# One two-bank PSUM tile for the sums of a feed-forward pair, and one VectorE operation of 1024 columns to read it

## The chip, the cores and the metric

The kernel runs on one core of a Trainium2 chip. The metric is device time of one execution in microseconds (us), as the median of several runs. A core has five engines with a queue each: TensorE (PE in the profile; its weight loads are listed apart as PEld), VectorE (DVE), ScalarE (ACT), GpSimd (POOL) and SyncE (SP). TensorE writes its results into PSUM, an accumulator memory of 128 partitions that is divided into banks; in this kernel a bank holds 512 fp32 numbers per partition. VectorE and ScalarE read PSUM; everything else lives in SBUF, and DMA queues carry it from and to HBM. Engines wait for one another through semaphores.

## The reference

The input x has the shape (4, 512, 128, 64): batch, time, F = 128 positions, H = 64 channels, in fp32. All arithmetic is fp32. There are two layers. The first is a chain of four residual blocks for each batch, with d = 128 * 64 = 8192 features per time step:

```python
xn = layernorm(x.reshape(b, t, d), g, b)
k, v, r = xn @ Wk, xn @ Wv, sigmoid(xn @ Wr)     # d -> 64
state = scan over time: decay * state + k * v
x = x + (r * states) @ Wo                        # 64 -> d
x = x + gelu(conv_F(layernorm(x)) + b)           # 3 taps over F, 64 -> 64 channels
x = x + layernorm(causal_depthwise_conv_T(layernorm(x)))   # 3 taps over time
x = x + (gelu(x @ W1 + b1) @ W2 + b2)            # 64 -> 256 -> 64, at each position
```

The second layer splits x into a moving average over 25 steps and the rest, takes the rest through a real Fourier transform over the 512 steps, mixes 128 modes with complex weights, transforms back, and adds the average. The change does not touch it.

## The kernel before, in words

The first layer holds data with features on partitions: a chunk is 128 features by 512 time steps, and a pair of chunks is a tile of [128, 2, 512]. One batch is 32 pairs (`NPR`). Six generator functions make the stages of a batch `b`:

- `project` (J, L325): k, v and r for all pairs, eight matmuls (L408) per pair.
- `scan` (Z, L421): the scan over time and the moments that follow from it. It is a chain of small steps that go from TensorE to VectorE or ScalarE and back.
- `attend_and_convolve` (A, L516): adds the attention's output (L530, L532), convolves over F (L565), and sums the pair and its squares over features with four matmuls into a PSUM bank `st` (`add_up`, L247 to L252, called from L598). `st` lives from the third pair of A to its end.
- `convolve_time` (C, L647): the time convolution on VectorE and ScalarE, with the same kind of sums in a bank of its own.
- `open_feed` (O, L707): spreads two columns of statistics to rows and makes the first two inputs of the feed-forward.
- `feed_forward` (F, L715): for each pair, and each quarter `q` of the 256 hidden channels, `widen` (four matmuls L733, then a gelu on ScalarE, L738) and `narrow` (four matmuls L746 that add into two PSUM banks). After the last quarter, VectorE adds bias and residual (L759), and `store` transposes the result (eight transposes L765), copies it out of PSUM (L773 or L778) and sends it to HBM. The store of a pair comes `lag` pairs after its sums: one in batches 0 and 1, two in batches 2 and 3. Batches 0 and 1 keep the result of the sums in `x4t` with three buffers of [128, 512], batches 2 and 3 in a spare tile of two chunks.

Three helpers recur in scan, C and O. `rows` (L281) turns a column of statistics into a row by four matmuls (`spread`, L239, L242) into a bank, and copies it out on ScalarE (L286). `finish` (L257) copies the sums of `add_up` to SBUF on ScalarE (L260), picks columns with small matmuls (L264) and copies them on VectorE (L269). `moments` (L271) makes mean and scale of them. The bank that `rows`, `finish` and the scan write is an argument: `of_a` takes half of the pool `ps_a`, `of_p` a bank of the pool `ps_p`.

[...]`ps_a`, `ps_c` and `ps_m` have one tile of two banks each; `ps_s` has one bank, which `st` of stage A and the second sum `pb` of the feed-forward share; `ps_p` has one bank, for `of_p`'s users (scan of batch 1, rows and sums of C and O in batches 0 to 2, and the preparation in batch 0) and the feed-forward's first sum `p`.

TensorE's order is written by hand: `in_turn` (L824) steps two chains of stages in turn, each by its share of the work: first batch 0's Z and A against batch 1's J and Z; then C0 against A1; O0 and F0 against J2 and Z2; C1 against A2; O1 and F1 against J3 and Z3; C2 against A3; O2 and F2 against C3 and O3; and F3 alone. A flag, `free_s`, keeps a feed-forward from starting while `st` is in use, and `feeding` keeps A's `st` from starting in a feed-forward. The order on the other engines is made by a scheduler when the kernel is built, and the builder puts in the semaphores, by the tiles that instructions read and write.

Of the kernel before, what the change touches and what calls it, by code (L numbers as in the profile page):

```python
# [10 lines left out]
F32 = mybir.dt.float32  # L11
AF = mybir.ActivationFunctionType
ALU = mybir.AluOpType
PSUM = bass.MemoryType.PSUM
# [66 lines left out]
def layer0(ctx, tc, dram, x, xt, vecs, wkvr, wo, wdec, wconv, fbias, w1, fb1, w2, fb2, x4):  # L81
# [16 lines left out]
    tiny = ctx.enter_context(tc.tile_pool(name="tiny", bufs=2))  # L98
    ps_a = ctx.enter_context(tc.tile_pool(name="ps_a", bufs=1, space=PSUM))
    ps_c = ctx.enter_context(tc.tile_pool(name="ps_c", bufs=1, space=PSUM))  # L100
    ps_s = ctx.enter_context(tc.tile_pool(name="ps_s", bufs=1, space=PSUM))
    ps_m = ctx.enter_context(tc.tile_pool(name="ps_m", bufs=1, space=PSUM))
    ps_p = ctx.enter_context(tc.tile_pool(name="ps_p", bufs=1, space=PSUM))

    def two(pool, tag):
        return pool.tile([P, 2, SL], F32, tag=tag, name=tag)
# [198 lines left out]
        return two(ps_a, "a")[:, 0, :]  # L305

    def of_p():
        return ps_p.tile([P, SL], F32, tag="p", name="p")

    projected = {}  # L310
    scanned = {}
# [13 lines left out]
    def project(b):  # L325
        pa = two(ps_m, "m") if b == 1 else two(ps_a, "a")
        held[0] = b == 1
        if b == 0:
            psum_w = ps_p.tile([P, SL], F32, tag="p", name="psum_w")
        stt = rowp.tile([P, NT, NS, 6], F32, tag="stt", name="stt")  # L330
        def token_major(i, xk):
            s, h = i // 2, i % 2 * 2
            nc.sync.dma_start(
                xk, x[b, h * P : (h + 2) * P, s * SL : (s + 1) * SL].rearrange("(t p) d -> p t d", p=P)
            )
            return xk

        def statistics(i, xk):
            s, h = i // 2, i % 2 * 2
            for t in range(2):  # L340
                stats = nc.vector.bn_stats(stt[:, h + t, s, :], xk[:, t, :])
                if b > 1:

                    tc.keep_in_program_order(stats)

        def weights(i):

            if i < NPR:
                w = spare("wx", 4 * S + SL).rearrange("p k n -> p (k n)")[:, 0 : 16 * S]
                w = w.rearrange("p (c s) -> p c s", c=4)  # L350
                nc.sync.dma_start(w, wkvr[2 * i : 2 * i + 4, :, 0 : 4 * S].rearrange("c p s -> p c s"))
                for k in range(2):
                    ws[i + k] = w[:, 2 * k : 2 * k + 2, :]

        def scale_weights(i, wq, pinned=False):
            for j in range(2):
                w = wq[:, j, 0 : 3 * S]
                scaled = nc.vector.tensor_scalar_mul(w, w, vec[:, G1, 2 * i + j : 2 * i + j + 1])
                if pinned:
                    tc.keep_in_program_order(scaled)  # L360

        ws, xps, xks = {}, {}, {}
        if b > 1:
            weights(0)
            for k in range(2):
                scale_weights(k, ws[k], True)
            xps[0] = load_x(b, 0)
        for i in range(NPR):
            first, last = i == 0, i == NPR - 1
            if b > 1:  # L370


                xks[i] = token_major(i, two(bk, "sq" if i % 2 else "x2"))
                if i % 2 == 0:
                    weights(i + 2)
                if not last:
                    xps[i + 1] = load_x(b, i + 1)
                wq, xp = ws.pop(i), xps.pop(i)
                for k in (i - 2, NPR - 2, NPR - 1) if last else (i - 2,):
                    if k in xks:  # L380
                        statistics(k, xks.pop(k))
            else:
                if unscanned[0]:

                    wq, xk = two(fr, "x1")[:, :, 0 : 4 * S + 3], spare("z", SL)
                else:

                    both = spare("wx", 4 * S + SL)
                    wq, xk = both[:, :, 0 : 4 * S], both[:, :, 4 * S :]
                n = 4 * S + 2 * (b == 0)  # L390
                nc.sync.dma_start(wq[:, :, 0 : n], wkvr[2 * i : 2 * i + 2, :, 0 : n].rearrange("c p s -> p c s"))
                xp = load_x(b, i)
                statistics(i, token_major(i, xk))
            if b == 0:
                nc.gpsimd.memset(wq[:, :, n:], 1.0)
                for j in range(2):
                    c = 2 * i + j

                    w = wq[:, j, :]
                    nc.tensor.matmul(  # L400
                        psum_w[0 : S + 2, 0 : 4 * S + 3], lhsT=w[:, 3 * S : 4 * S + 2], rhs=w,
                        start=c == 0, stop=c == NCH - 1,
                    )
            if b < 2:
                scale_weights(i, wq)
            for j in range(2):
                for k in range(2):
                    nc.tensor.matmul(  # L408
                        pa[:, k, :], lhsT=wq[:, j, k * P : (k + 1) * P], rhs=xp[:, j, :],
                        start=first and j == 0, stop=last and j == 1,  # L410
                    )
                if b > 1 and j == 1 and i + 2 < NPR:
                    scale_weights(i + 2, ws[i + 2], True)
                yield 1.0
        kvrg = rowp.tile([P, 2, SL], F32, tag="kvrg", name="kvrg")
        nc.scalar.copy(kvrg, pa)
        held[0] = False
        projected[b] = (kvrg, stt, psum_w) if b == 0 else (kvrg, stt)
# [97 lines left out]
    def attend_and_convolve(b):  # L516
# [62 lines left out]
        for i in range(NPR + 3):  # L579

            while begin[attend_and_convolve] < b + (min(i, 3) - 3) / 4:
                yield BLOCKED
            if i < 2:
                scaled(i)
            if i < NPR:
                attend(i)
                yield 1.0
            if 1 < i < NPR + 2:
                convolve(i - 2)
                yield 5.0  # L590
            while i == 3 and feeding[0]:
                yield BLOCKED
            if i == 3:
                st = ps_s.tile([P, SL], F32, tag="s", name="st")
                free_s[0] = False
            if i > 2:
                add_up(st, i - 3, *waiting.pop(i - 3), i == 3, i == NPR + 2)
                yield 1.0  # L598
            if b == 0 and i >= NPR and i < NPR + 2:
                begin[attend_and_convolve] = b + (0.25 if i == NPR else 0.75)  # L600
# [113 lines left out]

    def feed_forward(b):  # L715
        x3s = opened.pop(b)
        mids, x4s, obs, sums2 = {}, {}, {}, {}
        lag = 1 if b + 2 < B else 2
        turn = [0]
        while not free_s[0]:  # L720
# [17 lines left out]
            nc.scalar.activation(mid, pm, AF.Gelu_apprx_tanh, bias=fb1_sb[:, q : q + 1])  # L738

        def narrow(i, q):  # L740
            if q == 0:
                sums2[i] = of_p(), ps_s.tile([P, SL], F32, tag="s", name="pb")
            mid = mids.pop((i, q))
            for h in range(2):
                for j in range(2):
                    nc.tensor.matmul(  # L746
                        sums2[i][j][halves[h], :], lhsT=w2_sb[halves[j], q, :], rhs=mid[halves[j], h, :],
                        start=q == 0, stop=q == 3,
                    )
            if q < 3:  # L750
                return
            x3 = x3s.pop(i)
            if lag > 1:
                pair = spare("wx", 4 * S + SL)[:, :, 0:SL]
                x4s[i] = [pair[:, j, :] for j in range(2)]
            else:
                x4s[i] = [bk.tile([P, SL], F32, tag="x4t", name="x4t", bufs=3) for _ in range(2)]
            for j, pa in enumerate(sums2.pop(i)):
                nc.vector.scalar_tensor_tensor(x4s[i][j], pa, fb2_sb, x3[:, j, :], ALU.add, ALU.add)  # L759

        def store(i):
            pt = unit()
            for j, x4t in enumerate(x4s.pop(i)):
                for t in range(NT):
                    nc.tensor.transpose(pt[:, j, t * P : (t + 1) * P], x4t[:, t * P : (t + 1) * P], ident)  # L765
            s = i // 2
            if i % 2 == 0:
                obs[s] = bk.tile([P, NT, SL], F32, tag="ob", name="ob")
            o = obs[s][:, :, i % 2 * 2 * P : (i % 2 + 1) * 2 * P].rearrange("p t (j w) -> p j t w", j=2)
            pt = pt.rearrange("p j (t w) -> p j t w", t=NT)  # L770
            if i % 2:
                for h in range(2):
                    nc.scalar.copy(o[:, :, :, halves[1 - h]], pt[:, :, :, halves[h]])  # L773
                nc.gpsimd.dma_start(
                    x4[b][:, s * SL : (s + 1) * SL].rearrange("(t p) d -> p t d", p=P), obs.pop(s)
                )
            else:
                nc.scalar.copy(o, pt)  # L778
# [419 lines left out]
```

## Time and profile before

| | before |
|---|---|
| median of 3 runs | 3731.04 us (3726.51 to 3733.54) |
| profiled execution | 3727.17 us |
| its span in the profile | 3725.4 us |
| mean granted TensorE clock | 0.983 |
| TensorE busy | 3519.4 us, 94% |
| VectorE busy | 2671.6 us, 72% |
| ScalarE busy | 1779.8 us, 48% |
| GpSimd busy | 450.4 us, 12% |

A line such as "L759 DVE SCALAR_TENSOR_TENSOR x4t<-p,fb_sb,x 128x512" names the line of the kernel, the engine, the operation, the tile that is written and those that are read (by the program's names, which tiles share when they share memory), and its shape in partitions by columns. "Idle before" is how long the engine had nothing to do ahead of it, with the work that released it behind the arrow. The granted clock is the share of TensorE's full rate that the profile's clock records show. The stages follow one another in this way, in us from the start of the span: projections of batch 0 and what precedes A0 to about 430; scan of batch 1 beside A0 from about 446; C0 beside A1 from about 548 to 794; F0 beside J2 from 830, and its last pairs, with the scan of batch 2, to 1235; C1 beside A2 to 1462; F1 beside J3, and its last pairs to 1888; C2 beside A3 to 2114; F2 beside C3 from 2130 to about 2402, and the rest of F2 to 2490; F3 to 2745; the second layer to 3726.

### The profile page before, as it was taken

To read this page: it belongs to the slowest core of one execution; us is meant where nothing else is said; L and a number is where in the kernel's file an instruction comes from. 1 tells how busy PE (TensorE), PEld (TensorE's weight loads), DVE (VectorE), ACT (ScalarE), POOL (GpSimd) and SP (SyncE) were. 2 spreads that over 40 slices of the span, in tenths; PEclk is the share of its full clock that TensorE was granted. 3 is DMA by queue.
4 is the path that set the end of the run, shared out by engine and by line. 5 is a ranking of instruction groups with operands and counts; after the bars stand their busy time and mean duration, and the time that the engine had idled before them with its cause. 6 is when DMAs were issued, how large, how long until landed. Compare 5 with 4: busy or idle time off the path is not lost. (4 is left out here: it accounts for less than half of the span.)

```text
span 3725.4 us, 53006 instructions
## 1 busy us (share of the span) xinstructions
PE 3519.4 (94%) x20041; PEld 1366.8 (37%) x20041; DVE 2671.6 (72%) x3498; ACT 1779.8 (48%) x2331; POOL 450.4 (12%) x654
## 2 busy tenths in 40 slices
PE   9999999989999999999999989899989999899998
PEld 4433322224333223433322333333323843328433
DVE  4455569976777896677789699946658277792677
ACT  0013346546666565566656588878855200152100
POOL 0000012220011211001122122100000000001000
PEclk9999999999999999999999999999999999999999
DMA  9867647777885787788478677645569479994687
GB/s 313 282 211 243 227 154 270 254 264 259 293 295 176 249 275 267 265 292 296 167 240 286 210 245 268 233 154 194 199 202 285 154 231 295 300 295 167 214 286 263
DMA packets 427223, 910.29 MB, mean 244 GB/s; under 512 B 32728, under 2 KB 83160, under 8 KB 422872
## 3 DMA queue, kind: packets, MB, share of 16 engines
q1 hardware_dynamic: 353136, 636.92, 52.7%
q0 software_dynamic: 71680, 268.46, 19.8%
q8 instruction: 160, 2.62, 0.3%
q10 hardware_dynamic: 2152, 1.51, 0.1%
q14 instruction: 95, 0.78, 0.1%
HBM read 638.26 MB, written 268.50 MB: 243 GB/s over the span
## 5 line engine op out<-in xcount | busy, mean ns | idle before, releaser
L746 PE MATMUL p<-mid,w_sb 64*64 64x512 f32 x2048 | 560.8, 595 | 24.0 <-DVE wx L759 23.3
L746 PE MATMUL pb<-mid,w_sb 64*64 64x512 f32 x2048 | 533.4, 595 | 0.0
L738 ACT ACTIVATE mid<-c,fb_sb 128x1024 f32<-128x1024 f32 x256 | 284.6, 1112 | 94.5 <-PE c L733 92.3
L738 ACT ACTIVATE mid<-m,fb_sb 128x1024 f32<-128x1024 f32 x256 | 285.0, 1113 | 91.2 <-PE m L733 89.7
L733 PE MATMUL c<-x,w_sb 64*64 64x512 f32 x2016 | 281.6, 606 | 11.1 <-ACT mid L738 7.0
L733 PE MATMUL m<-x,w_sb 64*64 64x512 f32 x2016 | 283.3, 609 | 5.6 <-ACT ob L778 3.4
L746 PEld LDWEIGHTS p<-mid,w_sb 64*64 64x64 f32 x2048 | 160.4, 134 | 289.6 <-issue 244.0
L408 PE MATMUL a<-xp,wx 128*128 128x512 f32 x512 | 240.0, 613 | 6.6 <-issue 6.6
L1044 ACT COPY two<-a 128x512 f32<-128x512 f32 x64 | 37.5, 587 | 428.4 <-PE a L1039 428.4
L1067 PE MATMUL b<-xin,avg_sb 128*128 128x512 f32 x512 | 230.8, 593 | 3.3 <-DVE xin L1073 3.3
L1073 DVE TENSOR_TENSOR xin<-b,pm 128x512 f32<-128x512 f32 x256 | 159.1, 684 | 99.2 <-PE b L1070 84.3
L571 ACT ACTIVATE sq<-x 128x1024 f32<-128x1024 f32 x128 | 135.2, 1056 | 181.4 <-DVE x L568 181.3
L626 DVE SCALAR_TENSOR_TENSOR to<-kd,vec,to 128x510 f32<-128x510 f32 (+1 forms) x272 | 197.7, 747 | 10.5 <-ACT to L622 9.4
L701 ACT ACTIVATE kd<-kd,vec 128x512 f32<-128x512 f32 x256 | 193.1, 805 | 3.3 <-DVE kd L693 3.3
L252 PE MATMUL st<-x,ones 128*32 128x512 f32 x512 | 174.2, 611 | 10.7 <-DVE x L568 10.6
L926 DVE COPY xf<-b 128x256 f32<-128x256 f32 x128 | 54.4, 425 | 178.9 <-PE b L1013 170.0
L626 DVE SCALAR_TENSOR_TENSOR z<-x,vec,z 128x511 f32<-128x511 f32 x240 | 176.2, 747 | 5.0 <-ACT z L622 3.6
L704 DVE TENSOR_TENSOR x<-kd,kx 128x1024 f32<-128x1024 f32 x126 | 154.2, 1224 | 33.8 <-ACT kd L701 33.8
L532 DVE TENSOR_TENSOR x<-a,xp 128x1024 f32<-128x1024 f32 x128 | 156.3, 1221 | 29.8 <-PE a L530 27.3
L530 PE MATMUL a<-rst,wo_sb 64*128 64x512 f32 x512 | 148.6, 654 | 27.4 <-DVE x L532 25.4
L759 DVE SCALAR_TENSOR_TENSOR x4t<-p,fb_sb,x 128x512 f32<-128x512 f32 x64 | 47.8, 747 | 159.8 <-PE pb L746 157.4
L569 POOL DMA_DIRECT2D x<-x x128 | 93.5, 731 | 566.7 <-DVE x L568 561.7
(269 smaller groups left out, 6830.1 us busy)
## 6 DMA issues: line engine op xcount, KB each, us to landing
xp<-in_xt SPq DMA_DIRECT2D x256, 512.0 KB
kh<-to SPq DMA_DIRECT2D x156, 512.0 KB
x<-x POOLq DMA_DIRECT2D x128, 512.0 KB, 4.6
kx<-x SPq DMA_DIRECT2D x128, 512.0 KB
x<-ob POOLq DMA_DIRECT2D x64, 1024.0 KB, 8.1
xin<-x SPq DMA_DIRECT2D x64, 1024.0 KB
out<-xin POOLq DMA_DIRECT2D x64, 1024.0 KB, 5.9
x<-x SPq DMA_DIRECT2D x96, 512.0 KB
```

Of the source, the lines that this page charges most:

```text
L252: nc.tensor.matmul(st[32 * q : 32 * q + 32, :], lhsT=ones, rhs=src[:, j, :], start=first, stop=last,)
L408: nc.tensor.matmul(pa[:, k, :], lhsT=wq[:, j, k * P : (k + 1) * P], rhs=xp[:, j, :], start=first and j == 0, stop=last and j == 1,)
L530: nc.tensor.matmul(at[:, j, :], lhsT=wo_sb[js, :], rhs=rst[js, :], start=True, stop=True)
L532: nc.vector.tensor_tensor(x1, at, xp, ALU.add)
L626: tap = nc.vector.scalar_tensor_tensor(to[:, j, k:], xr[:, j, : SL - k], vec[:, w, c], to[:, j, k:], ALU.mult, ALU.add)
L701: tc.keep_in_program_order(nc.scalar.activation(d[:, j, :], d[:, j, :], AF.Identity, bias=vec[:, B4, c], scale=vec[:, G4, c]))
L704: nc.vector.tensor_tensor(x3, d, x2, ALU.add)
L733: nc.tensor.matmul(pm[halves[j], h, :], lhsT=w1_sb[halves[h], q * H : (q + 1) * H], rhs=x3[halves[h], j, :], start=True, stop=True,)
L738: nc.scalar.activation(mid, pm, AF.Gelu_apprx_tanh, bias=fb1_sb[:, q : q + 1])
L746: nc.tensor.matmul(sums2[i][j][halves[h], :], lhsT=w2_sb[halves[j], q, :], rhs=mid[halves[j], h, :], start=q == 0, stop=q == 3,)
L1067: nc.tensor.matmul(po[j], lhsT=avg_sb[:, j, :], rhs=xin[:, j, :], start=True, stop=False)
L1073: nc.vector.tensor_tensor(by_n(xin[:, j, :]), by_n(po[j]), by_c(pm[j % 2][:, j // 2, :]), ALU.add)
```

## The change

The two one-bank pools `ps_s` and `ps_p` go. A pool `ps_n` takes their place, with one tile `narrowed` of two banks, which is allocated once for the whole first layer. What took a bank from `ps_p` (`of_p`) now writes the first half of that tile, A's `st` is its second half, and the feed-forward's two sums are both halves. With the two sums in one tile, one VectorE operation of 1024 columns reads them in place of two operations of 512 each. Its result is one tile of two chunks; in batches 0 and 1 this is `x4t` with one buffer of [128, 2, 512] in place of three of [128, 512]. The lines of the new kernel stand one earlier up to `of_p`, one later from there to the feed-forward, and the sum is L757 in place of L759.

```diff
-    ps_s = ctx.enter_context(tc.tile_pool(name="ps_s", bufs=1, space=PSUM))
     ps_m = ctx.enter_context(tc.tile_pool(name="ps_m", bufs=1, space=PSUM))
-    ps_p = ctx.enter_context(tc.tile_pool(name="ps_p", bufs=1, space=PSUM))
+    ps_n = ctx.enter_context(tc.tile_pool(name="ps_n", bufs=1, space=PSUM))
...
     def of_p():
-        return ps_p.tile([P, SL], F32, tag="p", name="p")
+        return narrowed[:, 0, :]
+
+    narrowed = two(ps_n, "n")
...
         if b == 0:
-            psum_w = ps_p.tile([P, SL], F32, tag="p", name="psum_w")
+            psum_w = of_p()
...
             if i == 3:
-                st = ps_s.tile([P, SL], F32, tag="s", name="st")
+                st = narrowed[:, 1, :]
                 free_s[0] = False
...
-        mids, x4s, obs, sums2 = {}, {}, {}, {}
+        mids, x4s, obs = {}, {}, {}
...
         def narrow(i, q):
-            if q == 0:
-                sums2[i] = of_p(), ps_s.tile([P, SL], F32, tag="s", name="pb")
             mid = mids.pop((i, q))
             for h in range(2):
                 for j in range(2):
                     nc.tensor.matmul(
-                        sums2[i][j][halves[h], :], lhsT=w2_sb[halves[j], q, :], rhs=mid[halves[j], h, :],
+                        narrowed[halves[h], j, :], lhsT=w2_sb[halves[j], q, :], rhs=mid[halves[j], h, :],
                         start=q == 0, stop=q == 3,
                     )
...
             if lag > 1:
                 pair = spare("wx", 4 * S + SL)[:, :, 0:SL]
-                x4s[i] = [pair[:, j, :] for j in range(2)]
             else:
-                x4s[i] = [bk.tile([P, SL], F32, tag="x4t", name="x4t", bufs=3) for _ in range(2)]
-            for j, pa in enumerate(sums2.pop(i)):
-                nc.vector.scalar_tensor_tensor(x4s[i][j], pa, fb2_sb, x3[:, j, :], ALU.add, ALU.add)
+                pair = bk.tile([P, 2, SL], F32, tag="x4t", name="x4t", bufs=1)
+            x4s[i] = pair
+            nc.vector.scalar_tensor_tensor(pair, narrowed, fb2_sb, x3, ALU.add, ALU.add)
...
         def store(i):
             pt = unit()
-            for j, x4t in enumerate(x4s.pop(i)):
+            x4t = x4s.pop(i)
+            for j in range(2):
                 for t in range(NT):
-                    nc.tensor.transpose(pt[:, j, t * P : (t + 1) * P], x4t[:, t * P : (t + 1) * P], ident)
+                    nc.tensor.transpose(pt[:, j, t * P : (t + 1) * P], x4t[:, j, t * P : (t + 1) * P], ident)
```

## The prediction

> **What bounds the kernel now.** I began with the busy shares of the page:
>
> ```profile
> PE 3519.4 (94%) x20041; PEld 1366.8 (37%) x20041; DVE 2671.6 (72%) x3498; ACT 1779.8 (48%) x2331; POOL 450.4 (12%) x654
> ```
>
> TensorE (PE) bounds the whole, but the average hides the stages, so I cut layer 0 into stretches (columns: busy time of PE, PEld, DVE, ACT, POOL with instruction counts, PE clock, DMA share, GB/s):
>
> ```profile
> 446.00:548.00 102.00, 93.75 (x469) 30.37 (x467) 57.92 (x63) 41.02 (x59) 11.38 (x16) 0.93 0.46 155
> 548.00:794.00 246.00, 225.59 (x1131) 53.08 (x1131) 244.77 (x267) 153.70 (x210) 69.66 (x91) 0.99 0.77 261
> 830.00:1130.00 300.00, 296.90 (x2034) 119.12 (x2033) 218.42 (x293) 186.46 (x211) 27.13 (x32) 1.00 0.82 280
> 1130.00:1235.00 105.00, 91.35 (x622) 34.70 (x624) 73.28 (x95) 62.32 (x73) 12.94 (x17) 0.95 0.50 171
> 2130.00:2402.00 272.00, 242.86 (x1968) 100.75 (x1964) 267.65 (x302) 228.11 (x269) 58.95 (x70) 0.97 0.73 247
> 2490.00:2745.00 255.00, 253.86 (x2236) 100.49 (x2228) 150.49 (x150) 206.38 (x231) 11.32 (x15) 1.00 0.50 172
> ```
>
> The merged sum runs where a feed-forward does. Beside the projections (830 to 1130, and alike 1462 to 1790) and alone (2490 to 2745) TensorE is 99% busy. In F2 beside C3 (2130 to 2402) VectorE is full (267.65 of 272) and TensorE waits for it. Once the projections have ended (1130 to 1235; alike 1790 to 1888) TensorE has gaps. In 446 to 548 (scan(1) in A0) nothing is full: TensorE has gaps left by the scan's chain. Next the waits of two of them (us in total, times, longest):
>
> ```profile
> PE p L746 <- DVE wx L759: 20.9, 6, 5.5
> ...
> PE c L765 <- DVE x4t L759: 6.5, 4, 2.3
> PE m L765 <- DVE x4t L759: 2.0, 3, 0.9
> ```
>
> In F2/C3 the next pair's first matmul waits for the sum; in the tail (the lower two) the store's transposes wait for it. Last the groups by form (busy us, mean ns):
>
> ```profile
> L532 DVE TENSOR_TENSOR x<-a,xp 128x1024 f32<-128x1024 f32 x128 | 156.3, 1221 | 29.8 <-PE a L530 27.3
> L1051 DVE TENSOR_TENSOR pm<-even,a 128x512 f32<-128x512 f32 x256 | 158.2, 682 | 0.0
> L759 DVE SCALAR_TENSOR_TENSOR x4t<-p,fb_sb,x 128x512 f32<-128x512 f32 x64 | 47.8, 747 | 159.8 <-PE pb L746 157.4
> ```
>
> [...]two sums in a row start 0.66 us apart.[...]
>
> **The sum itself.** L1051 and L532 differ by 512 columns: 1221 - 682 = 539 ns. A sum of 1024 columns should be busy 0.745 + 0.539 = 1.284 us, and take a slot of 0.66 + 0.54 = 1.20. Two of 512 take 2 x 0.66 = 1.32 of slot, and 0.66 + 0.745 = 1.41 from start to end. So 0.125 us less per pair, at both measures; 128 pairs hold 16 us of VectorE work, most of it hidden. By stage:
>
> - F0 and F1 beside projections, F3, and F2's last eight pairs: the next work TensorE has (eight projection matmuls of 3.70 us in F0/F1; in F3 the store lies two pairs behind) covers the sum. F3's next pair starts 0.35 to 0.4 us after it in any case. Value: 0. Without the cover, at most 0.125 x 92 pairs = 11.5 us of gain.
> - F2/C3: 24 pairs have their sum here, each VectorE slot is on the path, since the sum starts about 2 us after its matmuls are done: 24 x 0.125 = -3.0 us.
> - The tails, lag 1: here the transposes of the first half begin after the first sum, while the second runs:
>
> ```profile
> 1156.92 0.75 DVE L759 SCALAR_TENSOR_TENSOR x4t<-p,fb_sb,x 128x512 f32<-128x512 f32 x1 [0.42 <-PE pb L746]
> 1157.59 0.74 DVE L759 SCALAR_TENSOR_TENSOR x4t<-pb,fb_sb,x 128x512 f32<-128x512 f32 x1
> ...
> 1157.82 1.22 PE L765 MATMUL m<-ident,x4t 128*128 128x128 f32 x8 [0.95 <-DVE x4t L759]
> ...
> 1158.97 1.09 PE L733 MATMUL c<-x,w_sb 64*64 64x512 f32 x8
> ```
>
> They begin 0.15 us after the first sum's end, and the next pair's work follows at 1158.97. With one sum all eight begin at 1156.92 + 1.284 + 0.15 = 1158.35, and eight in a row take 0.965 elsewhere: 1159.32, so 0.35 us later. Five pairs of a tail have such a gap (0.35, 0.38, 0.22, 0.35, 0.35: +1.65). In the last pair of F0 and F1 L532 stood between the two sums; behind one sum it comes after, and the second half is ready 0.65 earlier. Net +1.0 per tail, two tails: +2.0.
> - The single x4t buffer in place of three: the next pair's sum comes after this one's transposes anyway. 0. The waits dropped (TensorE on its own p and pb): four matmuls take 0.43 us with and without them. 0.
>
> **The single tile.** TensorE's order is written by hand, and in the built program is the same instruction for instruction; VectorE has 128 instructions fewer, and around the feed-forwards the same order otherwise; scan(1) and C0/A1 see shifts of at most five places on VectorE, ScalarE, POOL and SP (one SP load of weights goes two places up), among work that waits for TensorE: 0, at worst one of VectorE's slots, 1.2. But add_up's sums (st, now bank 1) and the users of of_p (bank 0) are now one tile, and the built program makes TensorE wait for readers of the other bank at ten places. Behind the waiting matmul stands all of TensorE's queue. One, in the trace before:
>
> ```profile
> 457.63 0.62 PE L252 MATMUL st<-x,ones 128*32 128x512 f32 x1
> ...
> 457.74 0.75 DVE L475 SCALAR_TENSOR_TENSOR wx<-rm,gw,p 128x512 f32<-128x512 f32 x1 [2.32 <-PE p L471]
> ...
> 458.63 1.13 PE L530 MATMUL a<-rst,wo_sb 64*128 64x512 f32 x4
> ```
>
> st was written at 457.63 while VectorE read p until 458.49; now st begins 0.1 after that: +0.95, and L530 and the rest after it. Likewise, reader's end against st's start:
>
> - scan(1), row copy L286 (450.41 against 449.68): +0.84; second L475 (465.36 against 464.50): +0.97; hs L499 (475.25 against 474.45): +0.9; sq L510 (482.66 against 482.32): +0.45, taken up by the 1.1 us gap before L242 at 484.49. The stage has slack on VectorE and DMA only, TensorE's chain to L497 (2.02 us wait) starts later as well, so they add: +2.7 with the one shown 3.66.
> - A1 with C0's rows: (541.62 against 540.93) +0.79, half of it hidden, as VectorE is about to be full: +0.4; the second copy ends before its st: 0.
> - C0's first add_up, after A1's copy of its sums (797.72 against 795.17): the copy itself waits for A1's last matmuls, then TensorE's L264 at 797.85 heads the chain to O0; about +0.9.
> - A3 with C2's me copy L269 (2102.44 against 2102.16): +0.38; with O2's row copy (2115.99 against 2114.81): +1.29, with the chain to O2 behind it (a 3.41 us gap before L242, then VectorE 2.0 us for the row).
>
> 3.66 + 0.4 + 0.9 + 0.38 + 1.29 = +6.6. Both ends: 0, where every one only eats a later gap, and 7.4 with the absorbed ones (+0.45, +0.39).
>
> **Sum.** -3.0 + 2.0 + 6.6 = +5.6 on the profiled execution's 3727.17 us (span 3725.4): 3732.8. The median of the runs, 3731.04, lies 3.9 above it: 3736.6, +0.15%.
>
> **Rivals.** *A: as summed*, own range 3732 to 3741. *C: the cross-bank waits vanish in later gaps*: -3.0 + 2.0 = -1.0, 3730. For it: 8.2 us of gaps in 446 to 548; against: the gaps end a chain that itself moves. *B: the clock*, the one that ends slower. The trace has stretches of 3.41 us (or multiples) with the granted clock at 0.5, some twenty after 430 us, several right behind a gap (a 2.31 us gap at 1171.3, then eight L733 matmuls in 1.99 instead of 1.09 us).[...] Each costs about 1.7 us; the 0.2% is passed from two more on (5.6 + 3.4 is over 7.5). Five longer gaps in each tail and five in scan(1) are candidates: 3741. Against: gaps of 1.33 and 3.2 us brought none. *B2: a 1024-column sum costs what two cost* (2 x 0.745 = 1.49): F2 +2.2 in place of -3.0, tails +2 more: about +13, 3744. Against it L532, which also reads two banks, at 1221 ns. *D: faster*: F2/C3's six TensorE waits shorten beyond the VectorE work and take four half-clock windows with them (2141.8, 2155.4, 2377.3 lie there): -3.0 - 6.8, with waits as in C: 3722. *E: the sum is not on the path anywhere* even in F2/C3, the rest as A: 3739.6, within B's time.
>
> **How the numbers follow.** Chances: A 0.40, C 0.11, B with E 0.31, B2 0.08, D 0.10. A measurement of this kernel can tell about 0.2% (7.5 us, its runs spread over 7) from no change: faster lies below 3723.6, slower above 3738.5. D is faster: 0.10. A and C are the same, 0.51, of which A's upper end is offset by E's lower. B and B2 are slower: 0.39. Leaving out D and the far half of B2 and of B, the range is 3727 to 3745.
>
> **What would show it.** In the profile after: L757 (the merged sum) x128 at 1.28 us and TensorE's waits on it in F2/C3 3 us less; transposes after one sum, with tail gaps of about 1.35 in place of 0.95; TensorE waits before st for L285, L475, L499 of near 0.9 us, and 446 to 548 longer by 3 to 4. Wrong if the sum lasts 1.4 or more, if A0 and A3 keep their length, or if the half-clock windows change by more than three.

## The result, and the profile after

| | before | after |
|---|---|---|
| median of 6 runs each | 3728.57 us | 3742.54 us (3733.15 to 3746.52) |
| profiled execution | 3727.17 us | 3742.59 us |
| its span | 3725.4 us | 3740.8 us |
| mean granted TensorE clock | 0.983 | 0.979 |

The ratio is 1.0034, with a 95% interval of 1.002 to 1.0048: slower by 7 to 18 us. That is inside the stated range (3727 to 3745), but not the likeliest case (A, 3736.6, "same"). The nearest is case B, 3741.

The page of the changed kernel shows the 128 VectorE instructions less and 15 us less VectorE work. TensorE is just as busy as before (3520.2 against 3519.4 us), so by the balance of the whole span the added time is TensorE's idle time; what half clock adds to its busy time is worked out further below.

```profile
span 3740.8 us, 52884 instructions
PE 3520.2 (94%) x20041; PEld 1346.3 (36%) x20041; DVE 2656.2 (71%) x3370; ACT 1777.8 (48%) x2331; POOL 447.6 (12%) x654
```

The merged sum costs what was worked out (1.284 us), by the groups by form; busy us and mean ns, and by its own view a median of 1283 ns:

```profile
L757 DVE SCALAR_TENSOR_TENSOR x4t<-n,fb_sb,x 128x1024 f32<-128x1024 f32 x64 | 81.9, 1279 | 162.6 <-PE n L745 162.6
```

TensorE's instructions are the same in both profiles, 20041 records in the same order, so they can be laid side by side one by one, and each stretch cut at the same instruction. Cut so, the table of stretches of the changed kernel shows (length in the second column, the clock third from the end):

```profile
451.89:559.52 107.63, 96.14 (x469) 32.01 (x462) 59.22 (x63) 41.40 (x60) 11.36 (x16) 0.90 0.44 150
842.91:1142.82 299.91, 296.89 (x2034) 119.13 (x2032) 215.40 (x269) 186.24 (x211) 27.09 (x32) 1.00 0.82 281
1142.82:1250.10 107.28, 90.16 (x622) 35.38 (x623) 72.29 (x87) 62.34 (x73) 12.25 (x17) 0.95 0.48 162
2147.20:2415.80 268.60, 235.47 (x1965) 79.94 (x1961) 265.53 (x278) 228.13 (x269) 60.09 (x69) 0.96 0.75 252
2505.16:2760.50 255.34, 252.93 (x2236) 96.94 (x2228) 146.45 (x118) 206.19 (x231) 11.36 (x16) 1.00 0.49 172
```

The same instructions took 101.9, 300.0, 104.8, 271.7 and (the fifth row, F3) 255 us before. The dense feed-forward and F3 did not move; F2 beside C3 is 3.1 us shorter; scan(1) in A0 is 5.7 longer and the first tail 2.5 (the second 2.0). That is 7.1 us of the 15.4 by which the span grew. Of the rest, 5.6 us lie in the first 446 us, where little has changed (they come back below), and the other 2.7 are spread in small pieces.

The waits of the first of these stretches, in the changed kernel (us in total, times, longest), and of the first tail:

```profile
PE n L251 <- DVE wx L476: 1.7, 2, 0.8
PE n L251 <- ACT rm L285: 1.4, 2, 0.7
PE n L251 <- DVE hs L500: 0.8, 1, 0.8
PE n L251 <- DVE sq L510: 0.3, 1, 0.3
```

```profile
PE c L764 <- DVE x4t L757: 6.9, 3, 2.8
PE m L764 <- DVE x4t L757: 4.5, 3, 1.5
```

None of the first four was there before: they are add_up's sums (bank 1) waiting for readers of the scan's bank (bank 0), six waits, 4.2 us. In the tail the transposes' waits for the sum grew from 8.5 to 11.4 us. One crossing in the timeline of the changed kernel, which answers to the one at 457.63 before:

```profile
464.07 0.75 DVE L476 SCALAR_TENSOR_TENSOR wx<-rm,gw,n 128x512 f32<-128x512 f32 x1 [2.32 <-PE n L472]
...
464.88 0.62 PE L251 MATMUL n<-x,ones 128*32 128x512 f32 x1 [0.84 <-DVE wx L476]
...
465.87 1.13 PE L531 MATMUL a<-rst,wo_sb 64*128 64x512 f32 x4
```

The matmul starts 0.06 us after the reader's end, and L531 still follows it by 1.0 us, as L530 did before: it is as late as the wait was long.

**Idle time, half clock and the rest.** TensorE's time in a stretch is busy time and idle time, and a part of the busy time is put down to the granted clock standing at 0.5. That loss is an estimate, half of the busy time inside such a window; it is near what the same work took at both clocks (eight L733 matmuls 1.09 us at full clock, 1.99 at 1172.44 in the kernel before). Both were worked out from the trace. Over the whole span idle time grew from 206.0 to 220.6 us, and half-clock loss from 53.9 to 65.7. The two can't simply be added, because TensorE was busy 7 us less in F2 beside C3. There VectorE sets the pace (busy 265.5 of 268.6 us in the changed kernel), and half clock is in good part hidden: the kernel before took 271.7 us with 6.2 us lost in one profile, and 270.7 with 11.3 lost in the other (e7). Where TensorE sets the pace, single profiles are best compared by length less half-clock loss. The table does it for three such stretches; its rows are the same instructions in each kernel.

| length less half-clock loss, us | before | before again (e7) | e3 | e2 | e6 | e5 | e11 | e1 | after | after again (e4) |
|---|---|---|---|---|---|---|---|---|---|---|
| tile in scan(1) and A0 | two | two | two | two | one | two | two | one | one | one |
| sum in F0 and F1 | 512 | 512 | 512 | 1024 | 512 | 512 | 512 | 512 | 1024 | 1024 |
| scan(1) in A0 (from 446) | 95.1 | 95.0 | 95.5 | 94.7 | 97.6 | 95.9 | 95.9 | 98.0 | 98.4 | 97.8 |
| tail of F0 (from 1130) | 99.7 | 99.7 | 100.1 | 102.4 | 100.1 | 100.7 | 100.4 | 100.3 | 102.2 | 102.8 |
| tail of F1 (from 1790) | 91.6 | 91.6 | 91.8 | 93.1 | 91.1 | 92.4 | 92.4 | 92.7 | 93.6 | 94.3 |
| all half-clock loss in the span | 53.9 | 61.2 | 49.8 | 73.8 | 62.5 | 66.4 | 64.3 | 68.1 | 65.7 | 71.0 |

### The profile page after: what moved, and what is told of

Same layout as the page of the kernel before. It is cut to its first block, busy times and chain, and to the rows that moved or that the text cites. A ratio compares the mean times of both kernels' runs of the same rounds, so it can differ in the third digit from the quotient of the medians.

```text
span 3740.8 us, 52884 instructions
## 1 busy us (share of the span) xinstructions
PE 3520.2 (94%) x20041; PEld 1346.3 (36%) x20041; DVE 2656.2 (71%) x3370; ACT 1777.8 (48%) x2331; POOL 447.6 (12%) x654
## 5 line engine op out<-in xcount | busy, mean ns | idle before, releaser
L745 PE MATMUL n<-mid,w_sb 64*64 64x512 f32 x4096 | 541.3, 597 | 27.5 <-DVE wx L757 27.5
L739 ACT ACTIVATE mid<-c,fb_sb 128x1024 f32<-128x1024 f32 x256 | 284.3, 1111 | 94.6 <-PE c L734 93.6
L734 PE MATMUL c<-x,w_sb 64*64 64x512 f32 x2016 | 271.8, 606 | 11.8 <-ACT mid L739 6.6
L734 PE MATMUL m<-x,w_sb 64*64 64x512 f32 x2016 | 273.7, 610 | 5.2 <-ACT ob L777 3.9
L745 PEld LDWEIGHTS n<-mid,w_sb 64*64 64x64 f32 x4096 | 157.5, 135 | 320.1 <-issue 269.9
L251 PE MATMUL n<-sq,ones 128*32 128x512 f32 x896 | 229.4, 610 | 2.8 <-ACT sq L572 1.9
L757 DVE SCALAR_TENSOR_TENSOR x4t<-n,fb_sb,x 128x1024 f32<-128x1024 f32 x64 | 81.9, 1279 | 162.6 <-PE n L745 162.6
L251 PE MATMUL n<-x,ones 128*32 128x512 f32 x512 | 173.2, 608 | 18.0 <-DVE x L569 12.3
L531 PE MATMUL a<-rst,wo_sb 64*128 64x512 f32 x512 | 149.9, 659 | 25.7 <-DVE x L533 23.7
```

The lines of the kernel that those rows point to most:

```text
L251: nc.tensor.matmul(st[32 * q : 32 * q + 32, :], lhsT=ones, rhs=src[:, j, :], start=first, stop=last,)
L531: nc.tensor.matmul(at[:, j, :], lhsT=wo_sb[js, :], rhs=rst[js, :], start=True, stop=True)
L734: nc.tensor.matmul(pm[halves[j], h, :], lhsT=w1_sb[halves[h], q * H : (q + 1) * H], rhs=x3[halves[h], j, :], start=True, stop=True,)
L745: nc.tensor.matmul(narrowed[halves[h], j, :], lhsT=w2_sb[halves[j], q, :], rhs=mid[halves[j], h, :], start=q == 0, stop=q == 3,)
```

## The experiments

Times are medians; ratios are to the kernel before on the same chip. A ratio is worked out from all executions and can differ a little from that of the medians. Theory T held that the loss is waits across banks and transposes that wait for the whole sum; the rival K that half-clock windows (stretches in which the granted clock stands at 0.5), which longer waits call up, make it.

**e1: one tile, two sums.** The tile of the changed kernel, the sums (and the three `x4t` buffers) of the kernel before:

```diff
-            nc.vector.scalar_tensor_tensor(pair, narrowed, fb2_sb, x3, ALU.add, ALU.add)
+            for j in range(2):
+                nc.vector.scalar_tensor_tensor(x4s[i][j], narrowed[:, j, :], fb2_sb, x3[:, j, :], ALU.add, ALU.add)
```

> The single tile of two banks stays, but each pair's sums are taken by two operations of 512 columns into two tiles, as before. Theory T (the loss is waits across banks plus transposes that wait for the whole sum): only the waits across banks remain, so TensorE's idle time in 446 to 548 is 3.2 us more than before, the two tails (1130 to 1235, 1790 to 1888) are as before, F2 beside C3 as before; in all +5 to +7 us, about 3735. Theory K (the loss is half-clock windows that any longer wait calls up): like the changed kernel in the first 548 us, +9 or more there, and about 3738. If the waits across banks cost nothing: 3729.

Measured: 3740.21 us, ratio 1.003 (1.0019 to 1.0041), about 11 us slower: above T's 5 to 7 us and nearer to K's 3738, though the first 548 us of its profile grew by 5 us and not by K's 9. The tile alone makes most of the change's loss. The waits are as T expected in scan(1): 2.8 us more idle than before. One thing was not expected: the tails, less half clock, are 0.6 and 1.1 us over those before, with two sums. It sits at the third pair, whose transposes start 0.8 us later against the instructions around them: there the second bank's last matmuls end 0.75 us after the first's, the first sum used to start in between (1182.33 us before, while pb was written until 1183.08), and over one tile it waits for both.

**e2: two tiles, one sum.** Pools of one bank outside the feed-forwards; at a feed-forward's start they are closed and one pool with a tile of two banks is opened, at its end the reverse:

```diff
+            banks("n")
...
+                sums2[i] = two(shared["n"], "n")
...
-            for j, pa in enumerate(sums2.pop(i)):
-                nc.vector.scalar_tensor_tensor(x4s[i][j], pa, fb2_sb, x3[:, j, :], ALU.add, ALU.add)
+                nc.vector.scalar_tensor_tensor(pair, sums2.pop(i), fb2_sb, x3, ALU.add, ALU.add)
...
+            banks("s", "p")
```

> Two tiles of one bank outside the feed-forwards, and one tile of two banks only while a feed-forward runs (the pools are closed and opened at its start and end); the sum is one operation of 1024 columns in all four. Theory T: 446 to 548 as before; tails longer by 2.0 to 2.5 us each, F2 beside C3 shorter by 3.1: +1.4, about 3730. Theory K: the longer waits of the tails call up half-clock windows too: +4 or more, 3733. If the waits across banks are not the larger part of the loss, this stays near the changed kernel's 3742.

Measured: 3732.06 us, ratio 1.0006 (0.9995 to 1.0017), 2 us, as T says (+1.4). The crossings are gone: the waits of its scan(1) in A0 are those before the change, and none names add_up's sums behind the scan (lines stand nine later here: L251 is what was L242 before, the spread of a row):

```profile
PE p L251 <- POOL rs L243: 2.1, 1, 2.1
PE p L506 <- DVE rst L501: 2.0, 1, 2.0
PE a L539 <- ACT rm L295: 1.4, 2, 0.7
```

The tails are longer by 2.6 and 2.6 us. e1's 11 and e2's 2 make up the change's 13 (its second series, e4, has 17, with 12 to 23): the tile is the larger part, the sum the smaller.

**e3: two tiles, one sum in batches 2 and 3 only.** As e2, with `merged = lag > 1`.

> As the kernel with two tiles outside the feed-forwards, but the merged sum only in batches 2 and 3, where the store lies two pairs behind; batches 0 and 1 keep two sums. Theory T: tails as before, F2 beside C3 shorter by 3.1: about 3725.5. Theory K says nothing of it beyond a change of windows by chance (3722 to 3732). If the merged sum gains nothing in F2 beside C3: 3729.

Measured: 3727.21 us, ratio 1.0 (0.9984 to 1.0015). The 3.1 us are in the profile (F2 beside C3 took 268.45 us, and its sums follow at 9.885 us a pair in place of 10.015, 0.13 less each), but in the time they can't be told from nothing.

**e4: the changed kernel again.**

> The changed kernel again, for a second profile. Theory T: the stretches whose idle time grew in the first profile grow by the same again (446 to 548 by 3.2, the tails by 3.5 and 3.0 us of idle, F2 beside C3 about 3 shorter in all); the first 446 us, which grew by 5.6, do not do so again, and the profiled time is nearer 3735. Theory K: the half-clock windows stand at the same places again and cost about 6 us more than in the kernel before; 3740 to 3744.

Measured: 3745.86 us, ratio 1.0047 (1.0032 to 1.0061). Scan(1)'s idle time grew by 2.75 and the tails' by 4.0 and 3.6, near T. But the time is K's or more (3740 to 3744), and so is the clock: half-clock loss is up by 17 us on the first profile of before, 7.9 of it in scan(1). F2 beside C3 was only 0.2 us shorter: its sums follow at 9.89 us again, but pairs in or behind a half-clock window took 10.1 to 10.5.

**e5, e11, e6: the tile in one part of the layer.** Two sums. In e5 two tiles until A1 begins its sums and one after; e6 is the complement: it starts with the one tile, and has `banks(*("s", "p"))` in this place.

```diff
+            if i == 3 and b == 1:
+                banks(*("n",))
```

> Two sums of 512 columns everywhere. Two tiles of one bank until A1 begins its sums, then the single tile of two banks to the end: the kernel with one tile and two sums, without the waits of scan(1) in A0. That kernel measured 0.30% (10 us) over the kernel before. Theory S (the waits in scan(1) make most of it, 2.8 us themselves and the rest by half-clock windows that they call up there): 0 to +3 us. Theory R (the loss is spread over all the crossings, at C0, A3 and O2 too): +5 or more.

> The complement: the single tile of two banks until A1 begins its sums, then two tiles; two sums of 512 columns everywhere. Theory S: +7 to +10 us, with 2.8 us more TensorE idle time in 446 to 548 and more time at half clock there than in the kernel before (6.8 us lost). Theory R: +3 to +5.

> Two tiles until A1, the single tile after, again, since the first time gave five runs only, 0.37% over the kernel before. Theory S or any sum over the crossings (C0 0.9, A3 0.4 and 1.3, times 1.5 for windows): +2 to +6 us. If it is +10 or more again, something in the later crossings costs more than the profile's idle time shows.

Measured: e5 3738.02 us, ratio 1.0037 (1.0025 to 1.005) on 5 runs; e11, the same kernel, 3736.03 us, 1.002 (1.0009 to 1.0032) on 22; e6 3731.36 us, 1.0018 (1.001 to 1.0027). So S falls, that scan(1) makes most of it: the loss is about half and half. e6's profile has the waits of scan(1), 2.2 us of added idle time, and costs 7 us. The later half costs some 7 us too, while its two profiles show only about 1.6 us less half clock in the tails, and nothing at the crossings of C0 and A3. The larger part of both is thus not in the waits that the profiles show; the part on the prediction comes back to it.

**e7: the kernel before again**, for the clock.

> The kernel before, for a second profile. If the half-clock windows stand where they stood (6.8 us lost in 446 to 548), the windows belong to the order of work and the extra ones of the changed kernel to its waits; if they stand elsewhere or are missing, they are chance, and single profiles can't be compared on them. Time within 0.2% of 3730.

Measured: 3725.72 us, 1.0002 (0.9993 to 1.0011). By the clock records the windows of the tails stood where they had stood, those in the first 446 us did not; half clock cost 61.2 us in the whole span, against 53.9. Up to 548 us, TensorE's work is the same in before, e7, e2, e3 and e8, and there half clock cost 13.7, 14.6, 22.9, 6.5 and 25.8 us. Scan(1) in A0 in e3 and in e8, the same instructions, by the table of stretches:

```profile
444.89:540.35 95.46, 87.22 (x470) 29.14 (x462) 56.96 (x62) 41.33 (x60) 11.47 (x16) 1.00 0.47 160
```

```profile
450.58:559.66 109.08, 100.84 (x470) 33.10 (x462) 58.03 (x63) 41.23 (x60) 11.48 (x16) 0.86 0.43 145
```

13.6 us between the two at clocks of 1.00 and 0.86: so a single profile can't say how many windows a change brings. The 5.6 us that the first 446 us of the changed kernel grew by are of this kind for the larger part (2.9 half clock).

**e8: the store two pairs behind in all batches.** On e2, to take the tails' waits away; in batches 0 and 1 the sum is written over its residual input x3:

```diff
-        lag = 1 if b + 2 < B else 2
+        lag = 2
-                    pair = bk.tile([P, 2, SL], F32, tag="x4t", name="x4t", bufs=1)
+                pair = spare("wx", 4 * S + SL)[:, :, 0:SL] if b + 2 >= B else x3
```

> Two tiles outside the feed-forwards, the merged sum in all four, and the store two pairs behind in batches 0 and 1 too; there the sum is written over its residual input (a fourth buffer for that)[...]. Theory T: the 8.5 us per tail that TensorE waited for sums before transposes are gone or nearly, F2 beside C3 is 3.1 shorter: 3730 - 17 - 3 = 3710, if nothing else comes due in the tails; if ScalarE or the scan's chain comes due in their place, 3718 to 3724. If the transposes' waits were hidden time: 3727.

Measured: 3732.12 us, ratio 1.0014 (1.0002 to 1.0027): a miss on every count. The waits of its first tail (us in total, times, longest) say where the 8.5 us went:

```profile
PE a L539 <- DVE x L541: 4.6, 2, 3.2
PE m L745 <- ACT mid L750: 4.0, 2, 3.7
```

No transpose waits for a sum any more, but a gelu and the attention's add come due in its place, and each tail is only 2.6 us shorter than before the change; A1 and A2 with C0 and C1 got longer by 1.5 and 1.7, and C2 with A3 by 4.6 us (the reordering and the fourth buffer were not tried apart). Time at half clock rose as well, by what the clock of every execution shows below.

**e9, e10: filling TensorE's waits.** If half clock follows waiting, work that fills the waits should drive it off. Spare matmuls whose results are overwritten, ahead of the longest waits (94 of them in e9, 104 in e10):

```diff
+    def fill(dst, n):
+        for _ in range(n):
+            nc.tensor.matmul(dst, lhsT=ident, rhs=decb, start=True, stop=True)
...
             pb = bank()
+            fill(pb, n if k == 0 else 0)
             spread(pb, col)
```

> The kernel before with spare matmuls of 128x512 (0.43 us each, 80 or so in all, their results overwritten) put ahead of TensorE's longest known waits: the scan's chain, the spreads of rows, the first projections of J2 and J3, the last six stores of F0 and F1, and 20 between the layers. They fill waits, so the order of the rest is unchanged. In the ten profiles so far every window of 3.41 us in which TensorE was busy under 40% was followed by one at half clock. If these windows cost time, some 33 of the 54 us that TensorE loses to half clock sit behind the filled waits: 15 to 25 us faster. If half-clock windows cost nothing in the end (other engines limit there), or the filling delays as much as it saves: 0 to +5 us.

> The changed kernel with the same spare matmuls (three in place of two ahead of the transposes in the tails, where its waits are longer). Theory W (of the 13 us that the change costs, 9 are longer waits and the rest half-clock windows that these waits bring): against the kernel before with the same filling it is 6 to 10 us slower, less than without filling. If the clock has no part in it: 13 us slower than that kernel. If all of it is the clock: no slower.

Measured: 3754.97 us, ratio 1.0076 (1.0059 to 1.0092), and 3772.36 us, 1.0118 (1.0099 to 1.0137). Both misses, for a flaw of the experiment: each spare matmul took two instructions and 0.87 us, not 0.43 (what one instruction of this shape takes in a row, 0.429 at L408 before), and the 20 between the layers alone cost 18 us. e10 is 17 us slower than e9, above W's 6 to 10, but W is not decided by that, since the changed kernel had more filling in its tails (20.8 us against 16.5 in each). In scan(1) in A0, where the filling was the same and half clock cost about as much (4.7 us against 4.5), e10 took 105.7 us against 100.4, and its idle time was 4.7 more: there the waits cost time without more of the half clock. What they do show is that half-clock windows can be driven off: in e9 the first tail lost 0 to half clock in place of 5.1 us, the second 1.7 in place of 6.5.

**e12: the filling in its right size**, on e3: 1 to 3 matmuls a wait, none between the layers. The trace and the edit have 30 of them, not the 23 of the expectation.

> The filling done again in the right size, on the kernel with two tiles and the merged sum in batches 2 and 3 (3727 us, level with the kernel before). In the profile of the filled kernels a spare matmul took two instructions and 0.87 us, twice what was reckoned, so each filling overran its wait, and the 20 between the layers held up the second layer's loads (18 us). Now there are 23, about half as many at each place, none between the layers: one or two per wait, never longer than the wait. If the half-clock windows behind these waits cost time: 10 to 15 us faster than the kernel without filling, 3712 to 3718. If they cost nothing in the end: 3724 to 3730. If a filling delays the work behind it even so: 3732 or more.

Measured: 3719.57 us, ratio 0.998 (0.9969 to 0.9992): 7.5 us (3 to 12) faster than the kernel before. e3, on another chip, was level with that kernel (ratio 1.0), so the filling brings about as much, under the expected 10 to 15. It beats both kernels. A filling in the first tail:

```profile
1149.97 0.59 PE L768 MATMUL pb<-mid,w_sb 64*64 64x512 f32 x2
1150.49 1.13 PE L292 MATMUL m<-decb,ident 128*128 128x512 f32 x2
1151.45 1.28 PE L797 MATMUL m<-ident,x4t 128*128 128x128 f32 x8
1152.67 1.09 PE L753 MATMUL c<-x,w_sb 64*64 64x512 f32 x8
```

The spare work ends just as the sum is ready, and the transposes follow without a wait. Half clock in the first layer outside F2 beside C3 cost 24 us, against 35 in e3, 46 and 41 in the two profiles of before.

## Why the prediction was right, and where it was wrong

The direction of A's sum and the range held; "same" as the likeliest class did not, because the time of B, which adds the clock, came out rather than that of A. The size of the sum did not hold either: it gave 5.6 us, and 13 were measured. The time is nearer to it (3742.5 against 3736.6) in part by luck, for the prediction started from a median of three runs, 2.5 us above that of six; and the range takes the result in because it was widened for the rivals B and B2, not by A, whose own range ended at 3741. Two of the signs that it named did speak against A: the profile of the changed kernel has 46 half-clock windows of 3.41 us in place of 37 (48 against 42 in the second profiles), where three more were allowed, and 446 to 548 grew by 5.7 us in place of 3 to 4, of which 3.3 are not half clock.

- *The sum itself.* 1.284 us predicted, 1.283 measured, so B2 falls. F0 and F1 beside projections and F3: 0 predicted, changes of 0.3 us or less measured.
- *F2 beside C3: -3.0.* Shown in size: -3.1 us in this profile, 0.13 us a pair. In the second profile, and in e2's, half-clock windows of 6.8 us took it back (271.5 us).
- *The tails: +2.0.* This term failed: 2.5 + 1.9 = 4.4 us less half clock in the profile, 3.1 + 2.7 in the second one, 2.7 + 1.5 in e2. The step from sum to transposes was right for four of six pairs (0.35 to 0.4 net, the first wait growing by 0.55). For the third the working gave 0.22 and 1.03 came: it took both banks to be done at the same time, and there the second was 0.75 us behind (its last matmul ended at 1183.08). The two sums before the change, and the one after it:

```profile
1182.33 0.75 DVE L759 SCALAR_TENSOR_TENSOR x4t<-p,fb_sb,x 128x512 f32<-128x512 f32 x1 [1.24 <-PE p L746]
1183.11 0.75 DVE L759 SCALAR_TENSOR_TENSOR x4t<-pb,fb_sb,x 128x512 f32<-128x512 f32 x1
1183.22 1.35 PE L765 MATMUL m<-ident,x4t 128*128 128x128 f32 x8 [0.15 <-DVE x4t L759]
```

```profile
1196.19 1.28 DVE L757 SCALAR_TENSOR_TENSOR x4t<-n,fb_sb,x 128x1024 f32<-128x1024 f32 x1 [2.02 <-PE n L745]
1197.62 1.06 PE L764 MATMUL m<-ident,x4t 128*128 128x128 f32 x8 [1.47 <-DVE x4t L757]
```

The last pair's gain of 0.65 is there at full clock (from the matmul before its transposes to the one behind them, 4.36 us in place of 5.02 in the first tail of e4 and the second of e2). In the first tail of this profile half clock ate it, behind a wait of 2.59 us:

```profile
1239.52 1.97 PE L764 MATMUL c<-ident,x4t 128*128 128x128 f32 x8 [2.59 <-DVE x4t L757]
```

The eight transposes took 1.97 us there, and 1.06 at full clock. So it was mainly the third pair that was mis-sized: 0.8 us in each of the two tails.

- *The single tile: +6.6.* In scan(1) with C0's first row copy, 3.66 + 0.4 predicted; the waits came one by one as priced (0.7 to 0.8 for each of five and 0.3), 4.2 us less 1.0 that the later waits for rst and rs gave back: 3.2. At C0 and A3, 0.9 + 0.38 + 1.29 predicted and nothing to be seen in the profile: 794 to 830 has 0.05 us more idle time, and 1888 to 2130 has 0.7, no more than e2, which has no crossings there (0.9). Rival C's mechanism, later gaps taking the waits up, was right for this half: in the kernel before, 4.05 us of gap stand before L408 there and 3.41 before L242.
- *What was left out of A's sum.* By idle time (scan), length less half clock (tails) and length (F2) the change costs 3.2 + 4.4 - 3.1, or some 4.5 us, in the first profile, and 2.75 + 5.8 - 0.2, or 8.3, in the second; the timed runs say 13 and 17. What is left, 8 or 9 us, fits half clock, as rival B said with two windows or more. Single profiles can't show it, but the record has the granted clock of every execution. Take one minus the mean clock, times the span: in 152 executions of the kernel before, in four series, this deficit and the time go up and down together (correlation 0.80, 0.62 us of time for each us of deficit). Against the kernel before in the same series, as means in us (good to 3 to 6):

| | e1 | e2 | e4, the changed kernel | e6 | e11 | e8 | e12 |
|---|---|---|---|---|---|---|---|
| deficit | +9.6 | +0.8 | +9.6 | +4.5 | +5.9 | +18.4 | -17.5 |
| time | +10.5 | +3.2 | +16.6 | +6.1 | +7.7 | +6.4 | -7.7 |

At 0.62 to 1 us each, half clock is 6 to 10 us of the changed kernel's loss; beside the waits it accounts in size for e1, for both halves of the tile's cost (e6, e11), and for a good part of what e8 failed to bring. That half clock follows waits is shown by e9 and e12, where waits were filled: e9's first tail lost 0 us to it in place of 5.1, and e12's mean deficit is 17.5 us below that of the kernel before. The split of the changed kernel's loss is an estimate from this correlation: e7, the same kernel as before, differs by 4.2 in deficit and 0.7 in time, and e10 failed to settle it.

## What to carry to other kernels

In this kernel two PSUM banks in one tile became one thing to whoever waits: check who reads the other bank before joining two pools for one wider operation, and count the first half's consumer too, which now waits for the second half. One operation in place of two paid here only where VectorE's slots were the path, 0.13 us for each of 24 of 128 pairs. By the estimate above TensorE's waits cost more than themselves here (of the 13 us lost, some 4.5 without half clock and the rest with it), and one to three spare matmuls in a known wait earned 7.5 us back here. Compare the granted clock of all executions, not of one profile.

## What the runs showed of the hardware

Half-clock windows came in a sharp pattern in these traces. In each of the fourteen profiles the half-clock stretches of the clock records begin on a grid of 3.413 us (to about 1 ns in before and after), whose phase differs from run to run: its first line lies 1.62 us behind the span's start in the profile of before, and 0.46 in that of after. Taking TensorE's busy share in each window of the grid, from the first clock record on, a full-clock window under 40% busy was followed by a half-clock window in 244 of 244 cases (33 of 33 in before and after), one between 40% and 50% in 58 of 106, one over 85% in 13 of 13040. Once at half clock it stayed there after 130 of 131 windows under 80% busy, and left it after 374 of 439 of the others. From these counts comes an estimate: a wait of over 0.6 x 3.41 = 2.05 us, or several shorter ones close together, would cost about 0.5 x 3.41 = 1.7 us more if it falls well into one window of the grid and TensorE sets the pace in the next. A phase left to chance would fit the spread of executions of one kernel (the kernel before from 3716 to 3744 us on one chip), but that was not shown: time and clock deficit of these executions do go together (correlation 0.80), but no run sets the phase.

A spare fp32 matmul of 128x128 by 128x512 into one bank took two instructions and 0.87 us in e9 (34 instructions in a row took 14.75 us from 2759.50 on): by this the 20 between the layers kept TensorE busy for some 17.4 us.
